# A written ScalarE order in the memory-attention stage of a fused two-layer kernel

## The chip, the cores and the metric

The kernel runs on one core of one Trainium2 chip. The metric is the device time of one execution in microseconds (us). Before the change it was 2856.61 us, the median of three runs (2856.53 to 2856.86).

The engines are named as the profile names them: PE is TensorE's matmul, PEld its weight load, DVE is VectorE, ACT is ScalarE, POOL is GpSimd, SP is SyncE.

## The reference, cut to what matters

The program adds six residual blocks to `x` (8 x 1024 x 256, float32), each after a layer norm: an FP4 feed-forward, an attention with decay, the FP4 feed-forward again, a ternary feed-forward, the memory attention, and the ternary feed-forward again. The change is in the memory attention (16 heads of 16, four memories):

```python
sq, sk = elu1(q), elu1(k)                     # elu1(x) = elu(x) + 1
out_m = einsum('bhsd,mhde->mbhse', sq, memories)
rel   = einsum('bhsd,mhd->mbhs', sq, memory_norms)
out_m = out_m / clip(rel, EPS, None)[..., None]
weights = softmax(rel.mean(axis=-1), axis=0)  # over the memories
mem_out = einsum('mbhse,mbh->bhse', out_m, weights)
kv_cum, k_cum = cumsum(sk x v), cumsum(sk)    # over the sequence
local = einsum('bhsd,bhsde->bhse', sq, kv_cum) / clip(sq . k_cum, EPS, None)
g = sigmoid(gate)
out = (g * mem_out + (1 - g) * local) @ w_o.T
x = x + out
```

## The kernel before, in words

**Tiling.** `x` stays on the chip. It is cut into NG = 16 groups of 512 rows, each of G = 4 tiles of 128 rows; two groups (GB = 2) or eight tiles (CB = 8) make one sequence. The stages run one after the other, and their ends overlap.

**The steps of memory attention.** `attn_memory` (the loop `for i in range(n + 5)`, n = 64) is a software pipeline by hand: step i works on tile i and on the five tiles before it, a = i-1 to e = i-5. With j = i mod 4, a step does in the code's order:

1. for tile b, memory product 0 (`remembered(0)`, tile pmo, L1410); for tile a, the four score products (`scored`, tile sc, L917), each for 32 of the 128 partitions; then memory products 1 to 3;
2. on VectorE, in between, the weighting of the memories (mo, L1423) and the masking of the scores (at, L926; the last one, `weigh_one(0)`, comes much later in the step);
3. for tile b, the product py (`recalled` L983, `weighed` L1001), copied to nt by ScalarE (L1515);
4. for tile a, the state (psd, then two ScalarE instructions, L1540); in each fourth step (j = 3) also the divisors of a later group (`divisors`: pr L1296, rt on ScalarE L1303 and on POOL L1304); the reciprocals rw (L1549);
5. the transposes of tiles d and c: pyt (L1565), copied by ScalarE to yt (L1567), and pn (L1572), from which VectorE makes y (L1575) and POOL adds four memories to it (L1582). In a fourth step pyt and pn are two halves of one bank, named pyn in the profile;
6. the running sum of the keys (kc, L1275), pieces of the layer-norm statistics (`ln.advance`, L206 to L228);
7. a projection of a later group (`project`: pk or pq, L1015; two ScalarE instructions to ee, L1255 and L1256; the ELU on VectorE, L1260), then the last masked score;
8. for tile e, the output product po (L1015); in a third step (j = 2) the transposes of the next group (`norm_turn`, L1235 and copies L1240);
9. `keys(i)`: for tile i, the transposed keys and the values in the tile pkv (L1378, L1015), and on ScalarE the copies vz (L1387) and kd (L1394) out of it and the two masked copies qz (L1398), which read sq alone; kd is left out in the last step of a sequence (i mod 8 = 7). The next step's scores read qz;
10. the ELU's last instruction, the addition of po to X (L1619), and in a second step (j = 1) the eight normalisations of a group (`norm`, L276 and L279).

A projection exists up to step 54.

**What sets the order.** The framework's scheduler orders the instructions of each engine; those handed to `pin` keep the order of the code on their engine. Before the change PE and DVE are pinned in this stage, ScalarE is not. PSUM has four banks that the stage calls `bank(0)` to `bank(3)` beside four score buffers.

**The statistics.** `statistics` cuts the layer-norm statistics into pieces: a mean and variance for each tile (L206, L207), and five pieces of terms for each batch of groups. `PLANS["memory"]` holds the batches and the step at which each is due. The first batch is done before the stage, in the last six groups of the ternary stage (`begin`); the others are spread over the steps before they are due. Before the change the batches have 3, 2, 3, 4 and 4 groups, due at 0, 1, 9, 21 and 37.

Of the kernel before, what the change touches and what calls it, by code (L numbers as in the profile page):

```python
# [9 lines left out]
F32 = mybir.dt.float32  # L10
# [7 lines left out]
P = 128  # L18
# [20 lines left out]
def macaron_kernel(  # L39
# [192 lines left out]
    def statistics(sizes, dues):  # L232

        mv = ln_pool.tile([P, NG * G, 2], F32, tag="ln_mv", name="ln_mv")
        lr = ln_pool.tile([P, NG * G], F32, tag="ln_r", name="ln_r")
        lb = ln_pool.tile([P, NG * G], F32, tag="ln_b", name="ln_b")

        def work(g0, size):  # L240

            out = []
            for n in range(G * g0, G * (g0 + size)):
                out.append(lambda n=n: tile_stats(X[n // G][:, n % G, :], mv[:, n, :]))
            n = slice(G * g0, G * (g0 + size))
            terms = []

            def term(k):
                if not terms:
                    terms.extend(norm_terms(mv[:, n, :], lr[:, n], lb[:, n]))  # L250
                terms[k]()

            return out + [lambda k=k: term(k) for k in range(5)]

        first, plan = [], {}
        begun = g0 = 0
        for size in sizes:
            size = min(size, NG - g0)
            if size <= 0:
                break  # L260
            shares, due = work(g0, size), dues[g0]
            if due <= begun:
                first += shares
            n, span = len(shares), due - begun
            for u in range(begun, due):
                plan[u] = shares[(u - begun) * n // span : (u + 1 - begun) * n // span]
            begun, g0 = due, g0 + size

        def advance(u):
            for share in plan.get(u, ()):  # L270
                share()

        def normalize(dst, g, only=None):
            for j in range(G) if only is None else (only,):
                n = G * g + j
                nc.scalar.activation(  # L276
                    dst[:, j, :], X[g][:, j, :], AF.Identity, bias=lb[:, n : n + 1]
                )
                nc.scalar.activation(dst[:, j, :], dst[:, j, :], AF.Copy, scale=lr[:, n : n + 1])  # L279

        return SimpleNamespace(
            mv=mv, lr=lr, first=first, advance=advance, normalize=normalize
        )
# [9 lines left out]
        "ternary": ((2, 2, 4, 4, 4), [max(0, g - 1) for g in range(NG)]),  # L293

        "memory": (
            (GB + 1, 2, 3, 4, NG), [max(0, G * (g - GB) - 3) for g in range(NG)]
        ),
    }
    begun = {}
# [902 lines left out]
    def attn_memory(after):  # L1202
        with ExitStack() as st:
# [18 lines left out]

            def norm(g):
                xn = xn_pool.tile([P, G, D], F32, tag="xn", name="xn")
                ln.normalize(xn, g)
                xns[g] = xn

            def norm_turn(g, banks, both_act=True):
                xt = bp.tile([P, 2, TG], F32, tag="xt", name="xt")
                xn = xns.pop(g)  # L1230
                for k in range(2):
                    pt = bank(banks[k], [P, TG], "pt")
                    for j in range(G):
                        pin(
                            nc.tensor.transpose(  # L1235
                                pt[:, j * P : (j + 1) * P], xn[:, j, k * P : (k + 1) * P], ident
                            )
                        )
                    if k == 0 or both_act:
                        nc.scalar.copy(xt[:, k, :], pt)  # L1240
                    else:
                        pin(nc.vector.tensor_copy(xt[:, k, :], pt))
                sq = bp.tile([P, 2, TG], F32, tag="sq", name="sq")
                sk = bp.tile([P, 2, TG], F32, tag="sk", name="sk")
                proj[g] = (xt, sq, sk)

            def project(g, m, of_q, pp):

                xt, sq, sk = proj[g]
                w, dst = (wq, sq) if of_q else (wkv, sk)  # L1250
                whole(
                    pin, pp, [(w[:, k, m * P : (m + 1) * P], xt[:, k, :]) for k in range(2)]
                )
                ee = lnp.tile([P, TG], F32, tag="ee", name="ee")
                nc.scalar.activation(ee, pp, AF.Relu, scale=-1.0)  # L1255
                nc.scalar.activation(ee, ee, AF.Exp, scale=-1.0)  # L1256

                def elu():
                    pin(
                        nc.vector.scalar_tensor_tensor(  # L1260
                            dst[:, m, :], pp, 0.0, ee, ALU.max, ALU.add
                        )
                    )
# [21 lines left out]
            def divisors(g, pr):  # L1285
# [17 lines left out]
                nc.scalar.activation(rt, pr[0 : NR + 32, :], AF.Identity, accum_out=su)  # L1303
# [4 lines left out]
            def weigh(b):  # L1308
# [21 lines left out]
                def exponents():  # L1330
# [11 lines left out]
                    nc.scalar.activation(lg, lg, AF.Exp)  # L1342

                def shares():
                    sm = cp.tile([P, 8, 2], F32, tag="sm", name="sm")
# [20 lines left out]

                return total, turned, exponents, shares

            def keys(i):
                g, j = divmod(i, G)  # L1370
                xt, sq, sk = proj[g][:3]
                cols = slice(j * P, (j + 1) * P)
                pkv = bank(3, [P, 2, D], "pkv")
                carried = (i + 1) % CB != 0
                if carried:
                    for m in range(2):
# [10 lines left out]
                nc.scalar.copy(  # L1387
                    vz[:, :, 0::2, :],
                    pkv[:, 1, :].rearrange("p (r e i) -> p r e i", e=2, i=HD),
                )  # L1390
                kd = None
                if carried:
                    kd = cp.tile([P, D], F32, tag="kd", name="kd")
                    nc.scalar.copy(kd, pkv[:, 0, :])  # L1394

                qz = cp.tile([P, 2, 2, P], F32, tag="qz", name="qz")
                for e in range(2):
                    nc.scalar.activation(  # L1398
                        qz[:, :, e, :], sq[:, :, cols], AF.Copy, scale=pm[:, e : e + 1]
                    )  # L1400
                chunk[i] = (vz, kd, qz)

# [30 lines left out]
            for i in range(n + 5):  # L1433
# [3 lines left out]
                if i == 0:  # L1437

                    waiting = []
                    for u in range(min(GB + 1, NG)):  # L1440
# [3 lines left out]
                        for v in range(G if u < GB else 1):  # L1444
                            pp = ps_s.tile([P, TG], F32, tag="sc", name="pq" if v % 2 else "pk")
                            waiting.append((project(u, v // 2, v % 2 == 1, pp), u, v))
                            if u < GB and u + 1 < NG:
                                ln.normalize(xns[u + 1], u + 1, v)
# [58 lines left out]
                if 0 <= b < n:  # L1507
# [7 lines left out]
                    nc.scalar.copy(nt, py)  # L1515
                    chunk[b] = (nt, mo, rw_b)
                if 0 <= a < n:

# [8 lines left out]
                if 0 <= a < n:  # L1527
# [8 lines left out]
                    if kd is not None:  # L1536

                        grown = sp.tile([P, 2, 2, HD], F32, tag="state", name="state")
                        for e_ in range(2):
                            nc.scalar.activation(  # L1540
                                grown[:, :, e_, :], pst[:, :, e_, :], AF.Copy,
                                scale=pm[:, e_ : e_ + 1],
                            )
                        if before is not None:
                            nc.gpsimd.tensor_tensor(grown, grown, before, ALU.add)
# [16 lines left out]
                if 0 <= d < n:  # L1562
                    y = ys.pop(d).rearrange("p (m h) i -> p m (h i)", m=2)
                    for m in range(2):
                        pin(nc.tensor.transpose(pyt[:, m, :], y[:, m, :], ident))  # L1565
                    yt = cp.tile([P, 2, P], F32, tag="yt", name="yt")
                    nc.scalar.copy(yt, pyt)  # L1567
                    ys[d] = yt
                if 0 <= c < n:
                    nt, mo_c, rw_c = chunk.pop(c)  # L1570
                    for m in range(2):
                        pin(nc.tensor.transpose(pn[:, m, :], nt[:, m, :], ident))  # L1572
                    y = cp.tile([P, H, HD], F32, tag="y", name="y")
                    pin(
                        nc.vector.tensor_tensor(  # L1575
# [14 lines left out]

                if "sum" in held:
                    running_sum(*held.pop("sum"))
                if i < n:
                    ln.advance(i)
                last = t + 1 if j == 3 else t
                elu = None
                if i < n and last < NG:
# [4 lines left out]
                weigh_one(0)  # L1602
                if 0 <= a < n:
                    chunk[a] = (vz, [ats[r] for r in range(4)], before, rw)
                if 0 <= e < n:
                    yt = ys.pop(e)
                    po = bank(1, [P, D], "po")
                    whole(pin, po, [(yt[:, m, :], wo[:, m, :]) for m in range(2)])
                if i < n and i % CB == 0:
                    mixing[1](bank(0, [P, NR], "pl"))  # L1610
                if i < n and j == 2 and t + 1 < NG:
                    norm_turn(t + 1, (3, 0))
                if i < n:
# [69 lines left out]
```

## Time and profile before

| what | value |
|---|---|
| median of three runs | 2856.61 us |
| the profiled execution | 2854.04 us |
| its span | 2851.3 us |
| mean granted TensorE clock | 0.984 |
| PE busy, 1972.1 to 2494.1 us | 484.5 of 522.0 us |
| DVE busy, 1972.1 to 2494.1 us | 422.1 of 522.0 us |
| ACT busy, 1972.1 to 2494.1 us | 268.4 of 522.0 us |
| POOL busy, 1972.1 to 2494.1 us | 252.7 of 522.0 us |

Times inside the profile are counted from the start of its span. The stretch in the table runs from the end of step 0's value products to that of step 55. A group's line says engine, source line, operation, output tile and input tiles. A wait's line says who waited for whom, the sum, the number of times and the longest.

### The profile page before, as it was taken

The page shows a single profiled execution, that of the slowest core. Times are in us where ns is not written, and L with a number is a line of the kernel's source. Part 1 is how long each engine was busy: PE and PEld are TensorE (multiplying, and loading weights), DVE is VectorE, ACT ScalarE, POOL GpSimd, SP SyncE. Part 2 cuts the span into 40 slices and gives each one's busy share as a digit, 9 for nine tenths or more (in the row PEclk, how much of TensorE's full clock was granted, in tenths as well). Part 3 has the DMA queues.
Part 4 walks back from the last instruction along what each step waited for, and adds up shares of the span by engine and source line. Part 5 has one row for each costly group of instructions (what it writes and reads, how often), then busy time and mean ns, then how long its engine had stood idle before and what let it go on. Part 6 is the DMA issues. An engine that isn't in the chain of part 4 may idle for free.

```text
span 2851.3 us, 53491 instructions
## 1 busy us (share of the span) xinstructions
PE 2644.8 (93%) x21536; PEld 1996.1 (70%) x21536; DVE 2089.3 (73%) x4732; ACT 1367.7 (48%) x3000; POOL 814.1 (29%) x760
## 2 busy tenths in 40 slices
PE   3779999999999998999999999998999999988999
PEld 2557777776676666677776779995666666667998
DVE  7787878776666667887878778555788877877654
ACT  3534444444434333444444456565455555435665
POOL 4434444430000002444444410001455455531000
PEclk9889999999999999999999999999999999999999
DMA  5100000000000000000000000000000000000011
GB/s 166 32 17 1 1 1 1 1 1 1 2 2 2 2 2 1 1 1 1 1 1 1 1 1 1 1 1 1 2 2 2 2 2 2 2 2 16 30 38 38
DMA packets 26228, 27.04 MB, mean 9 GB/s; under 512 B 5116, under 2 KB 25084, under 8 KB 25980
## 3 DMA queue, kind: packets, MB, share of 16 engines
q1 hardware_dynamic: 24838, 21.66, 2.4%
q8 instruction: 169, 2.77, 0.4%
q10 hardware_dynamic: 998, 1.44, 0.2%
q14 instruction: 79, 0.65, 0.1%
q0 software_dynamic: 144, 0.52, 0.1%
HBM read 15.23 MB, written 8.39 MB: 8 GB/s over the span
## 4 chain that ended last, share of the span: by engine, by line
PE 72%; DVE 16%; POOL 4%; ACT 4%; issue 2%; DMA 0%; POOLq 0%; DVEq 0%; ACTq 0%
PE po L874 9%; PE po L727 8%; PE ph L848 8%; PE pg L685 7%; PE pu L685 7%; PE py L1001 4%; PE sc L917 4%; PE po L1015 4%; PE pk L1015 4%; PE pkv L1015 3%; PE pq L1015 3%; DVE h L656 3%; PE py L983 2%; DVE qp L636 2%; DVE xn L656 1%
## 5 line engine op out<-in xcount | busy, mean ns | idle before, releaser
L727 PE MATMUL po<-wd,ht 128*128 128x256 f32 (+1 forms) x1536 | 359.9, 384 | 7.0 <-DVE x L736 6.5
L685 PE MATMUL pu<-wu,xt 128*128 128x352 f32 x1024 | 348.9, 463 | 11.0 <-DVE h L695 10.8
L685 PE MATMUL pg<-wg,xt 128*128 128x352 f32 x1024 | 348.5, 462 | 6.5 <-ACT sg L694 6.0
L727 PEld LDWEIGHTS po<-wd,ht 128*128 128x128 f32 (+1 forms) x1536 | 285.7, 193 | 45.1 <-DVE x L736 8.3
L660 POOL TENSOR_TENSOR h<-h,q_sc 128x704 f32<-128x704 f32 x128 | 177.5, 1387 | 451.9 <-DVE h L656 451.9
L685 PEld LDWEIGHTS pu<-wu,xt 128*128 128x128 f32 x1024 | 193.3, 192 | 114.5 <-DVE h L695 11.9
L695 DVE TENSOR_TENSOR h<-sg,pu 128x352 f32<-128x352 f32 x256 | 129.7, 516 | 187.4 <-PE pu L685 179.8
L685 PEld LDWEIGHTS pg<-wg,xt 128*128 128x128 f32 x1024 | 194.6, 191 | 100.2 <-ACT sg L694 10.9
L874 PE MATMUL po<-w,hl 128*128 128x256 f32 x1024 | 250.5, 282 | 1.1 <-DVE hl L859 1.1
L874 PE MATMUL po<-w,hh 128*128 128x256 f32 x1024 | 249.8, 282 | 0.0
L1582 POOL TENSOR_TENSOR y<-y,mo 128x256 f32<-128x256 f32 x256 | 210.2, 821 | 131.6 <-DVE y L1575 117.9
L656 DVE SCALAR_TENSOR_TENSOR h<-qp,h 128x704 f32<-128x704 f32 x256 | 227.2, 888 | 18.4 <-ACT qp L653 13.9
L859 DVE TENSOR_TENSOR hl<-hf,hh 128x512 fp32r<-128x512 f32 x256 | 168.0, 686 | 64.7 <-ACT hh L857 60.4
L848 PE MATMUL ph<-xh,w 128*128 128x512 f32 x512 | 203.6, 399 | 0.9 <-DVE x L1619 0.5
L694 ACT ACTIVATE sg<-pg 128x352 f32<-128x352 f32 x256 | 118.2, 462 | 177.7 <-PE pg L685 177.7
L848 PE MATMUL ph<-xl,w 128*128 128x512 f32 x512 | 200.6, 393 | 0.0
L644 POOL TENSOR_TENSOR h<-h,q_rs 128x704 f32<-128x704 f32 x128 | 177.6, 1387 | 71.4 <-DVE q_rs L640 54.2
L874 PEld LDWEIGHTS po<-w,hl 128*128 128x128 f32 x1024 | 195.0, 190 | 2.4 <-DVE hl L859 1.7
L874 PEld LDWEIGHTS po<-w,hh 128*128 128x128 f32 x1024 | 194.3, 190 | 1.8
L926 DVE TENSOR_TENSOR at<-sc,tri 128x512 f32<-128x512 f32 x256 | 171.4, 670 | 20.3 <-PE py L1001 17.2
L856 ACT ACTIVATE hf<-ph,b1c 128x512 f32<-128x512 f32 x256 | 167.7, 701 | 17.5 <-PE ph L848 17.4
L926 DVE TENSOR_TENSOR at<-sc,dec 128x512 f32<-128x512 f32 x256 | 158.5, 681 | 18.9 <-PE sc L917 18.9
(257 smaller groups left out, 5576.6 us busy)
## 6 DMA issues: line engine op xcount, KB each, us to landing
x<-in_x SPq DMA_DIRECT2D x15, 512.0 KB, 8.9
out<-x SPq DMA_DIRECT2D x15, 512.0 KB, 2.9
raw_w<-in_w_t SPq DMA_DIRECT2D x2, 1024.0 KB
wqkv<-in_wqkv_t SPq DMA_DIRECT2D x1, 768.0 KB
wu_n<-in_w_up ACTq DMA_DIRECT2D x2, 352.0 KB
wg_n<-in_w_gate SPq DMA_DIRECT2D x2, 352.0 KB
wd_n<-in_w_down ACTq DMA_DIRECT2D x1, 704.0 KB, 14.4
x<-in_x POOLq DMA_DIRECT2D x1, 512.0 KB, 10.9
```

The lines of the kernel that those rows point to most:

```text
L644: nc.gpsimd.tensor_tensor(vb, vb, rs[:, :, None].to_broadcast([P, nb, 16]), ALU.mult)
L656: nc.vector.scalar_tensor_tensor(v, mg, FP4_LEAST, v, ALU.max, op)
L660: nc.gpsimd.tensor_tensor(vb, vb, sc[:, :, None].to_broadcast(list(vb.shape)), ALU.mult)
L685: nc.tensor.matmul(ps, lhsT=xt[:, k, j * P : (j + 1) * P], rhs=w[:, k, cols], start=(k == 0), stop=(k == 1),)
L727: nc.tensor.matmul(po, lhsT=ht[:kn, c, :], rhs=wd[:kn, c, :], start=(c == 0), stop=(c == len(DCH) - 1),)
L848: nc.tensor.matmul(ph, lhsT=w1[:, k, f * P : (f + 1) * P], rhs=xt[:, k, :], start=(k == 0 and xt is xh), stop=(k == 1 and xt is xl),)
L856: nc.scalar.activation(hf, ph, AF.Gelu, bias=b1c[:, f : f + 1])
L859: nc.vector.tensor_tensor(hl[:, f, :], hf, hh[:, f, :].bitcast(F32), ALU.subtract)
L874: nc.tensor.matmul(po, lhsT=ht[:, f, j * P : (j + 1) * P], rhs=w2[:, f, :], start=False, stop=(f == NF - 1 and ht is hl),)
L926: nc.vector.tensor_tensor(at, sc.rearrange("p m (e t) -> p (m e) t", e=2), weight, ALU.mult)
L1015: nc.tensor.matmul(dst, lhsT=lhsT, rhs=rhs, start=n == 0, stop=n == len(parts) - 1)
L1582: nc.gpsimd.tensor_tensor(yv, yv, mo_c[:, :, :, m, :].rearrange("p r c n -> p c r n"), ALU.add)
```

## The change

All of it is in `attn_memory`, `normalize` and the plan. No arithmetic is changed.

- Every ScalarE instruction of the stage goes through `pin`, so ScalarE keeps the code's order too: in `normalize` (by a new argument), `norm_turn`, `project`, `divisors`, the exponents, `keys`, nt, the state and yt.
- The transposes pn come before the copy yt.
- `ln.advance(i)` moves from before the projection to behind the addition to X.
- The plan has batches of 5, 3, 4 and 4 groups, so that two more groups are done before the stage.
- In steps without a projection, the output product comes behind `keys` and not ahead of it, and pkv is in bank 2.

```diff
-            (GB + 1, 2, 3, 4, NG), [max(0, G * (g - GB) - 3) for g in range(NG)]
+            (GB + 3, 3, 4, NG), [max(0, G * (g - GB) - 3) for g in range(NG)]
...
-            def keys(i):
+            def keys(i, at):
...
-                pkv = bank(3, [P, 2, D], "pkv")
+                pkv = bank(at, [P, 2, D], "pkv")
...
                 vz = vzs[i % 4]
-                nc.scalar.copy(
-                    vz[:, :, 0::2, :],
-                    pkv[:, 1, :].rearrange("p (r e i) -> p r e i", e=2, i=HD),
+                pin(
+                    nc.scalar.copy(
+                        vz[:, :, 0::2, :],
+                        pkv[:, 1, :].rearrange("p (r e i) -> p r e i", e=2, i=HD),
+                    )
                 )
                 kd = None
                 if carried:
                     kd = cp.tile([P, D], F32, tag="kd", name="kd")
-                    nc.scalar.copy(kd, pkv[:, 0, :])
+                    pin(nc.scalar.copy(kd, pkv[:, 0, :]))
 
                 qz = cp.tile([P, 2, 2, P], F32, tag="qz", name="qz")
                 for e in range(2):
-                    nc.scalar.activation(
-                        qz[:, :, e, :], sq[:, :, cols], AF.Copy, scale=pm[:, e : e + 1]
+                    pin(
+                        nc.scalar.activation(
+                            qz[:, :, e, :], sq[:, :, cols], AF.Copy, scale=pm[:, e : e + 1]
+                        )
                     )
...
-                    yt = cp.tile([P, 2, P], F32, tag="yt", name="yt")
-                    nc.scalar.copy(yt, pyt)
-                    ys[d] = yt
                 if 0 <= c < n:
                     nt, mo_c, rw_c = chunk.pop(c)
                     for m in range(2):
                         pin(nc.tensor.transpose(pn[:, m, :], nt[:, m, :], ident))
+                if 0 <= d < n:
+                    yt = cp.tile([P, 2, P], F32, tag="yt", name="yt")
+                    pin(nc.scalar.copy(yt, pyt))
+                    ys[d] = yt
...
-                if i < n:
-                    ln.advance(i)
...
-                if 0 <= e < n:
+                def output():
                     yt = ys.pop(e)
                     po = bank(1, [P, D], "po")
                     whole(pin, po, [(yt[:, m, :], wo[:, m, :]) for m in range(2)])
+                    return po
+
+                if elu and 0 <= e < n:
+                    po = output()
...
                 if i < n:
-                    keys(i)
+                    keys(i, 3 if elu else 2)
                 if elu:
                     elu()
+                elif 0 <= e < n:
+                    po = output()
                 if 0 <= e < n:
                     xe = X[e // G][:, e % G, :]
                     pin(nc.vector.tensor_tensor(xe, po, xe, ALU.add))
+                if i < n:
+                    ln.advance(i)
```

More of the change, by code (lines that the diff above doesn't have):

```diff
@@ L271, in advance, with normalize @@
                 share()
-        def normalize(dst, g, only=None):
+        def normalize(dst, g, only=None, pin=lambda ins: ins):
             for j in range(G) if only is None else (only,):
                 n = G * g + j
-                nc.scalar.activation(
-                    dst[:, j, :], X[g][:, j, :], AF.Identity, bias=lb[:, n : n + 1]
-                )
-                nc.scalar.activation(dst[:, j, :], dst[:, j, :], AF.Copy, scale=lr[:, n : n + 1])
+                pin(
+                    nc.scalar.activation(
+                        dst[:, j, :], X[g][:, j, :], AF.Identity, bias=lb[:, n : n + 1]
+                    )
+                )
+                pin(
+                    nc.scalar.activation(
+                        dst[:, j, :], dst[:, j, :], AF.Copy, scale=lr[:, n : n + 1]
+                    )
+                )
         return SimpleNamespace(
@@ L1224, in norm @@
                 xn = xn_pool.tile([P, G, D], F32, tag="xn", name="xn")
-                ln.normalize(xn, g)
+                ln.normalize(xn, g, pin=pin)
                 xns[g] = xn
@@ L1239, in norm_turn @@
                     if k == 0 or both_act:
-                        nc.scalar.copy(xt[:, k, :], pt)
+                        pin(nc.scalar.copy(xt[:, k, :], pt))
                     else:
@@ L1254, in project @@
                 ee = lnp.tile([P, TG], F32, tag="ee", name="ee")
-                nc.scalar.activation(ee, pp, AF.Relu, scale=-1.0)
-                nc.scalar.activation(ee, ee, AF.Exp, scale=-1.0)
+                pin(nc.scalar.activation(ee, pp, AF.Relu, scale=-1.0))
+                pin(nc.scalar.activation(ee, ee, AF.Exp, scale=-1.0))
                 def elu():
@@ L1302, in divisors @@
                 su = bp.tile([NR + 32, 1], F32, tag="su", name="su")
-                nc.scalar.activation(rt, pr[0 : NR + 32, :], AF.Identity, accum_out=su)
+                pin(nc.scalar.activation(rt, pr[0 : NR + 32, :], AF.Identity, accum_out=su))
                 nc.gpsimd.tensor_scalar(rt, rt, EPS, 1.0, ALU.max, ALU.mult)
@@ L1341, in exponents @@
                     )
-                    nc.scalar.activation(lg, lg, AF.Exp)
+                    pin(nc.scalar.activation(lg, lg, AF.Exp))
                 def shares():
@@ L1386, in keys @@
                 vz = vzs[i % 4]
-                nc.scalar.copy(
-                    vz[:, :, 0::2, :],
-                    pkv[:, 1, :].rearrange("p (r e i) -> p r e i", e=2, i=HD),
+                pin(
+                    nc.scalar.copy(
+                        vz[:, :, 0::2, :],
+                        pkv[:, 1, :].rearrange("p (r e i) -> p r e i", e=2, i=HD),
+                    )
                 )
@@ L1393, in keys @@
                     kd = cp.tile([P, D], F32, tag="kd", name="kd")
-                    nc.scalar.copy(kd, pkv[:, 0, :])
+                    pin(nc.scalar.copy(kd, pkv[:, 0, :]))
                 qz = cp.tile([P, 2, 2, P], F32, tag="qz", name="qz")
                 for e in range(2):
-                    nc.scalar.activation(
-                        qz[:, :, e, :], sq[:, :, cols], AF.Copy, scale=pm[:, e : e + 1]
+                    pin(
+                        nc.scalar.activation(
+                            qz[:, :, e, :], sq[:, :, cols], AF.Copy, scale=pm[:, e : e + 1]
+                        )
                     )
@@ L1447, in attn_memory @@
                             if u < GB and u + 1 < NG:
-                                ln.normalize(xns[u + 1], u + 1, v)
+                                ln.normalize(xns[u + 1], u + 1, v, pin)
                             if len(waiting) > 1 or u == GB:
@@ L1514, in attn_memory @@
                     nt = cp.tile([P, 2, P], F32, tag="nt", name="nt")
-                    nc.scalar.copy(nt, py)
+                    pin(nc.scalar.copy(nt, py))
                     chunk[b] = (nt, mo, rw_b)
@@ L1539, in attn_memory @@
                         for e_ in range(2):
-                            nc.scalar.activation(
-                                grown[:, :, e_, :], pst[:, :, e_, :], AF.Copy,
-                                scale=pm[:, e_ : e_ + 1],
+                            pin(
+                                nc.scalar.activation(
+                                    grown[:, :, e_, :], pst[:, :, e_, :], AF.Copy,
+                                    scale=pm[:, e_ : e_ + 1],
+                                )
                             )
@@ L1572, in attn_memory @@
                         pin(nc.tensor.transpose(pn[:, m, :], nt[:, m, :], ident))
+                if 0 <= d < n:
+                    yt = cp.tile([P, 2, P], F32, tag="yt", name="yt")
+                    pin(nc.scalar.copy(yt, pyt))
+                    ys[d] = yt
+                if 0 <= c < n:
                     y = cp.tile([P, H, HD], F32, tag="y", name="y")
```

## The prediction, made before the result was known

> **What bounds the kernel now.** I read the page first, then the busy times of a stretch, then TensorE's waits, then two timelines of one step. The profiled execution took 2854.04 us, of which 2851.3 us are the span; the three timed runs have a median of 2856.61 us, 2.57 us above it. I add differences to the median.
>
> ```profile
> PE 2644.8 (93%) x21536; PEld 1996.1 (70%) x21536; DVE 2089.3 (73%) x4732; ACT 1367.7 (48%) x3000; POOL 814.1 (29%) x760
> ```
>
> TensorE (PE) is the bound overall. The change touches memory attention and its statistics alone. Step 0's value products (pkv, L1015) end at 1972.1 us and those of step 55 at 2494.1 us; the busy times of that stretch:
>
> ```profile
> core 0: us, PE busy (x) PEld busy (x) DVE busy (x) ACT busy (x) POOL busy (x), PEclk, DMA share, GB/s
> 1972.10:2494.10 522.00, 484.51 (x6297) 337.66 (x6296) 422.12 (x974) 268.38 (x691) 252.67 (x313) 0.98 0.01 2
> ```
>
> So 55 steps take 522.0 us, 9.5 us each; TensorE is busy for 93% of it, VectorE for 81%, ScalarE for 51%. TensorE's waits in it (engine, waiting line, releaser, sum, times, longest):
>
> ```profile
> PE pyn L1572 <- ACT yt L1567: 12.7, 13, 1.0
> PE sc L917 <- DVE at L926: 7.3, 7, 1.7
> PE pk L1015 <- DVE sq L1260: 5.4, 1, 5.4
> PE pmo L1410 <- DVE lg L1328: 4.6, 4, 3.1
> PE py L983 <- DVE mo L1423: 3.5, 7, 0.9
> PE pkv L1378 <- ACT xt L1240: 3.2, 13, 0.3
> ```
>
> These are 36.7 us of true idling. I also made a floor out of the cleanest steps, from the distance between successive value products in TensorE's timeline: 7.84 us for a first step of four (2385.80 to 2393.64), 8.35 for each eighth step, which has the mixing weights too (2421.87 to 2430.22), 7.87 for a second step (2475.47 to 2483.34, step 54, which has a second step's work), 9.20 for a third (2402.30 to 2411.50; it has the transposes of the next group), and 9.60 for a fourth (10.59 from 2375.21 to 2385.80, less its 0.98 us wait for yt). Steps 1 to 55 give 7 x 7.84 + 6 x 8.35 + 14 x 7.87 + 13 x 9.20 + 7.87 + 14 x 9.60 = 477 us. So 522.0 - 477 = 45 us of the stretch is waiting or a half clock: that is all that any reordering can win there.
>
> **Which order ScalarE keeps now.** The four lines below are ScalarE's timeline after the value products of step 43, the next three TensorE's at the same place (start, us, engine, line, tiles).
>
> ```profile
> 2386.86 0.37 ACT L1387 COPY vz<-pkv 128x256 f32<-128x256 f32 x1 [0.69 <-PE pkv L1015]
> 2387.13 0.38 ACT L1394 COPY kd<-pkv 128x256 f32<-128x256 f32 x1
> 2388.37 0.91 ACT L1398 ACTIVATE qz<-sq,pm 128x256 f32<-128x256 f32 x2 [0.86 <-PE pmo L1410]
> 2390.14 0.37 ACT L1515 COPY nt<-py 128x256 f32<-128x256 f32 x1 [0.86 <-PE py L1001]
> ```
>
> ```profile
> 2385.80 1.03 PE L1015 MATMUL pkv<-wkv,xt 128*128 128x256 f32 x4
> 2386.76 0.37 PE L1410 MATMUL pmo<-memb,sq 32*128 32x128 f32 x1
> 2386.77 0.50 PE L917 MATMUL sc<-qz,sk 32*128 32x256 f32 x3
> ```
>
> The score products sc of the next step start at 2386.77, at the heel of the value products. They read qz, the two masked copies that `keys` writes last. The qz pair shown, at 2388.37, comes after those scores have begun, so it isn't theirs: it is the next step's, waiting only until its buffer is read. ScalarE has been running this pair about a step ahead of where the code writes it (in the timeline's beginning four such copies, from 1956.9, stand before the first vz at 1972.17). That lead is what lets TensorE pass from pkv to sc with no pause.
>
> **The change, part by part.**
>
> *Written ScalarE order.* No instruction is added, and no DMA on SP's, ScalarE's or POOL's queue is moved. The pins put vz, kd, qz, qz in this order behind each step's pkv; TensorE's own order (pkv, memory product 0, scores) is pinned already. So the scores of a step now wait for: vz starting 0.03 us after pkv's modelled end (2386.83 to 2386.86), 0.27 to kd, 0.27 to the next instruction (ScalarE passes from a kd at 2376.71 to a normalisation at 2376.98), 0.91 for the pair, and some 0.05 from a ScalarE end to TensorE's start (yt ends at 2382.67, pyn starts at 2382.72): 1.53 us after pkv's end, where they now start 0.06 before it. That is **1.59 us a step**. Only memory product 0 lies beside it. Queued behind are all of TensorE's later products, so VectorE's masked scores and POOL's sums come later too. Upper side: 1.59. Lower side: memory product 0 (four passes of about 0.11, 0.43 in all) leaves the score block, but the three other row groups still have 4 score and 4 memory passes each, so I take nothing off; if it counted in full, 1.16. It holds for the 55 steps with a projection (0 to 54); six of them have no kd (0.27 less): 55 x 1.59 - 6 x 0.27 = **+85.8 us**.
>
> In the second step of four the eight normalisations (L276, L279, 0.40 apart, 3.2 us) now stand between qz and nt. From the scores' start to the end of py are 3.27 us (2386.77 to 2390.04), so nt is not late; if that cover is gone, at most 0.3 x 13 = 4 us. What the order takes away: normalisations no longer sit in ScalarE's queue waiting for statistics, ahead of vz; pmo's 4.6 us wait (longest 3.1) follows from that.
>
> *Shared transposes ahead of their copies.* In 13 fourth steps pyt and pn share a bank, and TensorE sits 0.98 us between them until yt is copied. Now both pairs go first: **-12.7 us**. yt comes 0.3 later, hidden behind the 1.7 us projection that stands before po.
>
> *Statistics at a step's end; five groups before the stage.* Each tile costs VectorE 0.53 us (L206 and L207). Behind the X addition, they no longer hold up the last masked score (sc <- at, 7.3 us) or the ELU. The 13 pieces of step 0 ran from 1971.23 to 1978.35 and cost TensorE 5.4 us at pk, and then half a clock (four pk passes took 3.80 us at 1979.13 where a clean step has 1.72); they now run in the ternary stage's last groups, where VectorE is busy for 24.8 of 60 us (1900 to 1960) and TensorE for 57.7. I cost them at nothing there; were the cover gone, 7.1 us.
>
> *Keys ahead of the last output products.* From step 55 there is no projection. po (1.03 us) then covers most of the qz wait, and po's own wait for the reciprocal (about 0.6 a step) moves off. These steps already turn in 7.87 us on a circle through POOL's four additions (3.15 us), mo, py and y, with TensorE idle about 0.7 before py; I take 0, between -5 and +4.
>
> **The sum.** If the 1.59 us pause makes every other wait of the stretch vanish (none but step 1's and three of 1.7 to 3.1 is longer, and those have their cause removed), then 85.8 - 45 = **+41 us**. The clock comes on top. In these slices the granted clock is the third number from the right (0.50 is half):
>
> ```profile
> 2011.68:2015.09 3.41, 2.21 (x38) 1.68 (x35) 3.34 (x10) 0.69 (x3) 3.00 (x4) 1.00 0.00 0
> 2015.09:2018.51 3.42, 3.42 (x65) 2.84 (x58) 1.53 (x4) 1.19 (x6) 0.32 (x1) 0.50 0.03 7
> ...
> 2318.87:2322.29 3.42, 1.77 (x20) 1.00 (x18) 3.25 (x9) 0.58 (x3) 2.44 (x3) 1.00 0.00 0
> 2322.29:2325.70 3.41, 3.34 (x80) 2.74 (x80) 2.88 (x9) 2.48 (x7) 1.27 (x1) 1.00 0.01 2
> ```
>
> A gap of 1.20 us before a score product (at 2013.45) was followed by a 3.4 us slice at half clock; one of 1.72 (at 2322.36) was not. Those gaps stood among thin score products; the new pause stands behind 3.7 us of dense ones (projection, po, pkv). Bounds: 0 to 37 such slices (two of three such gaps, of 55), each losing at most 1.7 us, 0 to 63 us; I take 4, near 0: +7.
>
> The page "TensorE: Matmul & The Clock Gate" of the Trainium skill, in its section "HAM oscillation — how this bites in real kernels", asks only that gaps stay under about 3.4 us. By that rule the new pauses would cost no clock and the sum would stay at +41; the slice at 2015.09 speaks against it.
>
> Forecast: 2856.61 + 41 + 7 = **2904 us** (+1.7%).
>
> **The rivals.**
>
> *The waits stay.* The pause moves VectorE and POOL with it, and only what is taken away by the edit itself goes (12.7 + 5.4): +68 us, with 8 half-clock slices (+14) +82: 2938. For it: y, its POOL additions and mo form a circle, and VectorE's share is high. Against: that circle turns in 7.87 us and a step would take 9.4.
>
> *The masked copies stay ahead: faster.* One mechanism, at L1398: if the scores find qz ready as they do now, the 45 us go and nothing comes: 2812. It decides at 45 / 55 = 0.82 us a step; under that pause the kernel is not slower. For it: ScalarE is idle half the time and qz needs nothing of pkv. Against: a queue in the written order can't reach qz before kd is done, and kd waits for pkv.
>
> *The order is not what changes:* pins that agree with the order already kept, 2857 within 6. Against: 1956.9 before 1972.17.
>
> **How the numbers follow.** Forecast 0.70 (own range 2874 to 2923: pauses of 1.16 us and no slice give +17, ten slices, the late nt and the tail's 4 give +66), waits stay 0.17, masked copies ahead 0.08, no change 0.05. 8 in 10 asks for the first two almost whole: 2874 to 2938. Slower by over 0.2% (5.7 us, about what a measurement can tell from no change) 0.87, within it 0.05, faster 0.08.
>
> **What would show it.** In the changed profile qz follows kd at 0.27 us and no longer waits for PE; a new wait "sc <- ACT qz" of about 1.5 us stands some 55 times; pyn <- yt and the 5.4 us at pk are gone; a plain step takes 9.4 us; VectorE's share falls. I am wrong if sc still starts at pkv's end, or if most slices behind a pause run at half clock (then up to 2960).

## The result, and the profile after

The changed kernel takes 2902.59 us (median of 4 runs, 2900.68 to 2903.37), the kernel before in the same comparison 2856.74 us: a ratio of 1.0158, 95% interval 1.0141 to 1.0176. The profiled execution took 2902.0 us, with a span of 2900.3 us and a mean granted clock of 0.984, the same clock as before.

The page's line of busy times, then the busy times of the stretch from the end of step 0's value products to that of step 55 (the columns are those of the same table before):

```profile
PE 2670.1 (92%) x21536; PEld 2018.9 (70%) x21536; DVE 2092.4 (72%) x4717; ACT 1369.9 (47%) x3000; POOL 812.7 (28%) x760
```

```profile
1980.10:2536.90 556.80, 495.94 (x6290) 350.42 (x6289) 418.80 (x938) 268.97 (x691) 249.79 (x311) 1.00 0.01 2
```

No engine has more instructions. The 55 steps take 556.8 us, where they took 522.0. Of the 34.8 us more, 23.4 are idle time of TensorE and 11.4 busy time (495.94 against 484.51): memory product 0, which ran among the scores, now runs alone in front of them. VectorE is busy for 418.80 / 556.80 = 75% of them, down from 81%. The clock in the stretch is 1.00, up from 0.98. TensorE's waits in the stretch (sum, times, longest):

```profile
PE sc L923 <- ACT qz L1407: 48.9, 55, 1.5
PE pn L1581 <- ACT nt L1525: 4.5, 12, 0.6
PE pkv L1384 <- ACT xt L1246: 3.8, 13, 1.0
PE py L989 <- DVE mo L1433: 3.1, 4, 1.1
```

One new wait stands 55 times, and four of the six old lines are gone: pyn for yt, sc for the masked scores, pk for the ELU, pmo for lg. Those for xt (3.8 us) and mo (3.1 us) stay, and one for nt (4.5 us) is new. ScalarE's timeline behind the value products of a plain step, then TensorE's at the same place:

```profile
2428.17 0.37 ACT L1394 COPY vz<-pkv 128x256 f32<-128x256 f32 x1 [0.69 <-PE pkv L1021]
2428.43 0.38 ACT L1402 COPY kd<-pkv 128x256 f32<-128x256 f32 x1
2428.70 0.92 ACT L1407 ACTIVATE qz<-sq,pm 128x256 f32<-128x256 f32 x2
2433.03 0.37 ACT L1525 COPY nt<-py 128x256 f32<-128x256 f32 x1 [3.42 <-PE py L1007]
```

```profile
2427.10 1.03 PE L1021 MATMUL pkv<-wkv,xt 128*128 128x256 f32 x4
2428.06 0.71 PE L1420 MATMUL pmo<-memb,sq 32*128 32x128 f32 x4
2429.67 1.17 PE L923 MATMUL sc<-qz,sk 32*128 32x256 f32 x16 [0.90 <-ACT qz L1407]
```

The qz pair now follows kd and waits for nothing but its turn. The value products end at 2427.10 + 1.03 = 2428.13 and the scores start 1.54 us later, where they used to start 0.06 us before that end: 1.60 us a step. So it is in 46 of the 55 steps. The six steps without kd have 1.32 or 1.33, and three of the first five have 1.66 to 1.75. The wait's own sum (48.9) is smaller than 55 x 1.60 because it counts only true idling; the 0.71 us of memory product 0 lie beside it.

Where the difference lies, from the ends of the value products in both traces (the two profiled executions, 48.0 us apart; the medians are 45.9 apart):

| part of the span | before | after | difference |
|---|---|---|---|
| up to step 0's value products | 1972.1 | 1980.2 | +8.0 |
| steps 1 to 55 | 522.0 | 556.7 | +34.7 |
| steps 56 to 63 | 64.6 | 67.5 | +2.9 |
| the rest | 292.6 | 295.9 | +3.3 |
| span | 2851.3 | 2900.3 | +49.0 |

The first row lies in the loop ahead of step 0. Its new wait, in TensorE's waits from 1930 to 1980 us:

```profile
PE pt L1241 <- ACT xn L282: 6.9, 4, 3.0
```

The transposes of the first groups wait for normalisations that ScalarE now takes in the code's order, behind other work of that loop.

### The profile page after: what moved, and what is told of

The parts are those of the page before. It is cut to its first block, busy times and chain, and to the rows that moved or that the text cites. A ratio compares the mean times of both kernels' runs of the same rounds, so it can differ in the third digit from the quotient of the medians.

```text
span 2900.3 us, 53369 instructions
## 1 busy us (share of the span) xinstructions
PE 2670.1 (92%) x21536; PEld 2018.9 (70%) x21536; DVE 2092.4 (72%) x4717; ACT 1369.9 (47%) x3000; POOL 812.7 (28%) x760
## 3 DMA queue, kind: packets, MB, share of 16 engines
q10 hardware_dynamic: 998, 1.44, 0.2%
## 4 chain that ended last, share of the span: by engine, by line
PE 71%; DVE 14%; ACT 8%; POOL 4%; issue 2%; DMA 0%; POOLq 0%; DVEq 0%; ACTq 0%
PE po L880 8%; PE po L733 8%; PE ph L854 8%; PE pg L691 7%; PE pu L691 7%; PE py L1007 4%; PE sc L923 4%; PE pk L1021 4%; PE po L1021 4%; PE pkv L1021 4%; PE pq L1021 3%; DVE h L662 3%; DVE qp L642 2%; PE py L989 2%; DVE xn L662 1%
## 5 line engine op out<-in xcount | busy, mean ns | idle before, releaser
L862 ACT ACTIVATE hf<-ph,b1c 128x512 f32<-128x512 f32 x256 | 167.3, 698 | 17.5 <-PE ph L854 17.4
```

Of the source, the lines that this page charges most:

```text
L862: nc.scalar.activation(hf, ph, AF.Gelu, bias=b1c[:, f : f + 1])
```

## The experiments

Times are medians; each ratio is to the kernel before, measured beside it on the same chip. "First step" to "fourth step" are the steps with j = 0 to 3, as in the prediction; their lengths are means over steps 12 to 52. The kernel before had medians of 2856.74 to 2857.64 us beside the runs, so differences between runs of different comparisons carry about 1 us. The theory tested first: the pause behind kd is the whole loss, and it hides the waits of before.

### 1. The masked copies a step earlier

The changed kernel, with the pair of qz for step i + 1 written behind the scores of step i:

```diff
+            def masks(i):
...
                 for r in (...):
                     scored(r)
+                if i == 0:
+                    masks(0)
+                if i + 1 < n:
+                    masks(i + 1)
```

> The changed kernel with the masked copies qz written (and pinned) one step earlier, behind the score products of the step before, where ScalarE ran them before the change; nothing else differs. Theory (the pause of 1.59 us between the value products and the scores, at 55 steps, is the loss): 86 us go, about 10 of VectorE's and POOL's waits come back, so about 2826 us, and no wait of sc for qz. Rival (the written order as a whole costs, by nt, state, rt and yt): under half of it goes, above 2860.

Measured: 2867.32 us, ratio 1.0032 (1.0020 to 1.0045). The pause is gone, and 35.3 of its 86 us come back. In its place, in the same stretch (525.4 us long), two other waits stand:

```profile
PE py L989 <- DVE mo L1440: 26.9, 29, 2.2
PE pn L1592 <- ACT nt L1536: 17.1, 12, 2.1
```

The second is the eight normalisations of a second step, which stand ahead of nt (in one step they run from 2180.32 on, and nt starts at 2184.91): in the changed kernel the pause held up py as well, so they cost less there (4.5 us). The first is a wait of before (3.5 us there) that has grown. So the pause costs time, but less than its length: something else was waiting behind it.

### 2. The masked copies ahead of vz and kd

The changed kernel, with the pair written first in `keys`, so that it runs while TensorE is still at the value products:

```diff
+                qz = cp.tile([P, 2, 2, P], F32, tag="qz", name="qz")
+                for e in range(2):
+                    pin(nc.scalar.activation(qz[:, :, e, :], ...))
                 vz = vzs[i % 4]
...
-                qz = cp.tile([P, 2, 2, P], F32, tag="qz", name="qz")
-                for e in range(2):
-                    pin(nc.scalar.activation(qz[:, :, e, :], ...))
```

> The changed kernel with qz written ahead of vz and kd inside keys; ScalarE stays pinned. Theory: qz then ends 2.2 us after the start of the ELU's first copy, some 0.3 us behind the value products in three steps of four and not at all in a third step, so about 15 of the 86 us stay and about 2840 us result. Rival (the copies vz and kd, now later, become the late ones): state products wait, and it stays above 2860.

Measured: 2855.26 us, ratio 0.9993 (0.9984 to 1.0003). One place in the queue is worth 47.3 us, the whole loss, and yet 15 us less than the expectation. In its profile, of an execution of 2860.19 us, steps 1 to 55 take 514.4 us, 7.6 less than before; step 0's value products still end 7.1 us later than before, and steps 56 to 63 take 68.2 us, 3.6 more. TensorE's largest wait in steps 1 to 55:

```profile
PE py L989 <- DVE mo L1433: 21.2, 28, 2.2
```

Again py's wait for the weighted memories. Its cause is looked for in the fifth, ninth and twelfth run.

### 3. The pause alone

The kernel before, with only vz, kd and qz pinned:

```diff
-                nc.scalar.copy(vz[:, :, 0::2, :], ...)
+                pin(nc.scalar.copy(vz[:, :, 0::2, :], ...))
...
-                    nc.scalar.copy(kd, pkv[:, 0, :])
+                    pin(nc.scalar.copy(kd, pkv[:, 0, :]))
...
-                    nc.scalar.activation(qz[:, :, e, :], ...)
+                    pin(nc.scalar.activation(qz[:, :, e, :], ...))
```

> The kernel before with only vz, kd and qz pinned on ScalarE, nothing else of the change. Theory: the pause of 1.59 us comes alone (+86 us), and the waits of VectorE for POOL and of TensorE for at and mo, 27 of the 45 us, vanish behind it: about 2915 us. Rival (these waits stay beside the pause): about 2942 us. Third view (the loss needs the whole ScalarE order): near 2857 us.

Measured: 2924.97 us, ratio 1.0235 (1.0219 to 1.0250). The three pins alone cost 67 us, more than the whole change, between the theory's 2915 us and the rival's 2942. TensorE's waits in the stretch:

```profile
PE sc L917 <- ACT qz L1401: 53.1, 52, 3.5
PE pyn L1576 <- ACT yt L1571: 12.7, 13, 1.0
PE pmo L1414 <- DVE lg L1328: 4.6, 4, 3.1
...
PE py L983 <- DVE mo L1427: 0.2, 1, 0.2
```

The wait for mo vanishes behind the pause without any edit to it; those for yt and lg stay whole. So the pause swallows some of the old waits, and the rest of the change had to take away the others.

### 4. Output products behind the keys in every step

The changed kernel, with po always behind `keys`, so that 1 us of TensorE's work covers most of the pause:

```diff
-                if elu and 0 <= e < n:
-                    po = output()
...
                 if elu:
                     elu()
-                elif 0 <= e < n:
+                if 0 <= e < n:
                     po = output()
```

> The changed kernel with the output products po behind keys in every step, not in the last ones alone, so that 1.03 us of TensorE work lie between the value products and the scores. Theory: the pause falls from 1.59 to 0.56 us at 55 steps, 57 us less: about 2846 us. Rival (the pause isn't what bounds, or the later addition to X delays memory product 1, which shares its bank with po): 2890 us or more.

Measured: 2876.96 us, ratio 1.0066 (1.0051 to 1.0081), 25.6 us faster than the changed kernel instead of 57. The expectation was too high from the start: of the pauses only 48.9 us were idle, the rest already held memory product 0. In its stretch sc waits for qz only 5.4 us (5 times), but pkv waits 12.4 us for xt, 13 times: by the code's order, po was what covered the copies of the next group's transposes in each third step. And py waits 8.3 us for mo.

### 5. The shared transposes alone

The kernel before, with the transposes pn ahead of the copy yt:

```diff
                         pin(nc.tensor.transpose(pyt[:, m, :], y[:, m, :], ident))
-                    yt = cp.tile([P, 2, P], F32, tag="yt", name="yt")
-                    nc.scalar.copy(yt, pyt)
-                    ys[d] = yt
                 if 0 <= c < n:
...
                         pin(nc.tensor.transpose(pn[:, m, :], nt[:, m, :], ident))
+                if 0 <= d < n:
+                    yt = cp.tile([P, 2, P], F32, tag="yt", name="yt")
+                    nc.scalar.copy(yt, pyt)
+                    ys[d] = yt
```

> The kernel before with the shared transposes ahead of the copy yt, and nothing else of the change. Theory of the prediction (the 0.98 us wait at 13 fourth steps is on the path): 12.7 us less, about 2844 us. Rival, formed after the first runs (in a fourth step POOL does rt, the state and four additions, 5.4 us, before the next step's mo can be written, so TensorE only meets the wait one step later, before py): pyn no longer waits for yt, but py waits for mo some 0.7 us more in each first step; 2853 to 2857 us.

Measured: 2854.16 us, ratio 0.9988 (0.9979 to 0.9997): 2.8 us and not 12.7. The edit did what it says: the wait for yt is gone, and a fourth step takes 9.34 us instead of 10.54, 13 x 1.20 = 15.6 us less. But the first step behind it takes 9.10 us instead of 8.09, 13 x 1.01 = 13.1 us more. POOL's timeline across that boundary, then VectorE's line and TensorE's line behind it:

```profile
2384.45 1.92 POOL L1304 TENSOR_SCALAR rt<-rt 96x512 f32<-96x512 f32 x1 [3.91 <-ACT rt L1303]
2386.45 0.32 POOL L1545 TENSOR_TENSOR state<-state 128x64 f32<-128x64 f32 x1
2386.73 3.15 POOL L1584 TENSOR_TENSOR y<-y,mo 128x256 f32<-128x256 f32 x4
```

```profile
2389.91 0.42 DVE L1423 TENSOR_TENSOR mo<-pmo,rw 128x256 f32<-128x256 f32 x1 [1.57 <-POOL y L1584]
```

```profile
2390.39 0.64 PE L983 MATMUL py<-sq,state 32*32 32x128 f32 x16 [0.82 <-DVE mo L1423]
```

In a fourth step POOL clips rt (1.92 us) ahead of the state and the four additions. The additions end at 2389.88, VectorE's mo follows, and only then py. TensorE arrives sooner and waits for POOL instead of for yt: py's waits for mo rise from 3.5 to 11.5 us. This chain, which runs from one step into the next, is what is called POOL's circle below.

### 6. The statistics alone

The kernel before, with the new batches and the pieces at the step's end:

```diff
-            (GB + 1, 2, 3, 4, NG), ...
+            (GB + 3, 3, 4, NG), ...
...
-                if i < n:
-                    ln.advance(i)
...
                     pin(nc.vector.tensor_tensor(xe, po, xe, ALU.add))
+                if i < n:
+                    ln.advance(i)
```

> The kernel before with the new plan (five groups ahead of the stage) and the statistics at a step's end, and nothing else of the change. Theory of the prediction: the 5.4 us wait at pk and its half clock go (about 5 us in all), and the 7.3 us of sc waiting for at: about 2845 us. Rival (the statistics' later place holds up mo of the next step, and py with it): py waits for mo more by what sc waits less; about 2852 us.

Measured: 2843.68 us, ratio 0.9950 (0.9938 to 0.9963), 13.2 us faster. Nothing shows in the ternary stage: step 0's value products end at 1971.6 us (1972.1 before). The waits at pk (5.4 us), for the last masked score (7.3, now 0.3) and of pmo for lg (4.6) are gone, the last with ScalarE still free. But another has grown from 3.5 us, as the rival said:

```profile
PE py L983 <- DVE mo L1423: 17.6, 22, 2.2
```

So TensorE idles almost as long as before in steps 1 to 55 (36.4 us, 37.5 before). The profiled stretch is 10.4 us shorter, and 8.4 of that lie in steps 1 to 4: step 1, with the wait at pk and the half clock behind it, took 12.65 us and now takes 4.43. In steps 5 to 55 the profile shows a gain of 2.1 us. The first part of the theory holds; the masked scores' 7.3 us were not won, their place was taken by mo.

### 7. The first loop's normalisations free

The changed kernel, with the normalisations of the loop ahead of step 0 left to the scheduler:

```diff
-                                ln.normalize(xns[u + 1], u + 1, v, pin)
+                                ln.normalize(xns[u + 1], u + 1, v)
```

> The changed kernel with the normalisations of the loop ahead of step 0 not pinned on ScalarE; all else as changed. Theory (written between the ELU's copies they come late for the transposes: pt waits 6.9 us for xn, and step 0's value products end 8.0 us later than before): 6.5 us of that come back, about 2896 us. Rival (the 8 us come from the two more groups of statistics ahead of the stage): no difference, 2902 us.

Measured: 2897.26 us, ratio 1.0138 (1.0124 to 1.0152): 5.3 us less than the changed kernel. Step 0's value products end at 1972.3 us again. So the +8.0 us of the table's first row is this pin; the steps gave 2.8 us of it back (559.5 against 556.7 us).

### 8. Masked copies first, normalisations in halves

The second kernel with the first loop free, the eight normalisations split over the second and third step behind yt, and po ahead of the keys again:

```diff
-                ln.normalize(xn, g, pin=pin)
+                for v in (2 * q, 2 * q + 1):
+                    ln.normalize(xns[g], g, v, pin)
...
-                if elu and 0 <= e < n:
+                if 0 <= e < n:
                     po = output()
...
-                    keys(i, 3 if elu else 2)
+                    keys(i, 3)
```

> As the run with qz first (2855 us), and with: the first loop's normalisations not pinned; a group's eight normalisations written in halves behind yt in the second and third steps, in place of all behind qz; po ahead of keys in the last steps again. Theory (pn waits for nt in third steps, the first loop and the last steps cost 6, 6.5 and 3 us): about 2840 us. Rival (POOL's circle, rt, state, four additions, mo, py, sets the step and takes back what is won elsewhere): 2848 us or more.

Measured: 2851.54 us, ratio 0.9977 (0.9968 to 0.9987), 3.7 us less than the second kernel. The steps keep their mean lengths (first step 9.08 us, 9.09 in the second kernel; third step 10.15, 10.21), and py still waits 21 us for mo. Nor is ScalarE's order out of play:

```profile
PE sc L923 <- ACT qz L1396: 10.5, 10, 2.4
```

In each eighth step (i mod 8 = 1) the first half of the normalisations comes late, and qz behind it: the third step that follows takes some 10.5 us, every other one some 9.8, where the second kernel has 10.2 for both. What the halves won in one they lost in the other. In the profiles the gain lies outside: step 0's value products end 5.9 us sooner than in the second kernel and steps 56 to 63 take 4.6 us less, while steps 1 to 55 take 3.2 us more.

### 9. The transposes, with POOL's clipping late

The fifth kernel, with the clipping of rt behind the four additions on POOL:

```diff
-                nc.gpsimd.tensor_scalar(rt, rt, EPS, 1.0, ALU.max, ALU.mult)
+                clips.append(rt)
...
                         pin(nc.gpsimd.tensor_tensor(yv, yv, mo_c[...], ALU.add))
+                for rt_ in clips:
+                    pin(nc.gpsimd.tensor_scalar(rt_, rt_, EPS, 1.0, ALU.max, ALU.mult))
+                clips.clear()
```

> As the run of the kernel before with the transposes alone (2854 us), and POOL's clipping of rt (1.92 us, needed some steps later) written behind the four additions in fourth steps and pinned there. Theory (POOL's circle rt, state, additions, mo, py took back what the transposes won): the first step falls from 9.10 to about 8.0 us, 13 times, so about 2842 us. Rival (the first step is held by something else, VectorE's masked score or the state's copies): no change, 2854 us.

Measured: 2846.13 us, ratio 0.9961 (0.9948 to 0.9973). Against the kernel before, the transposes and the late clipping together are worth 11.1 us; the transposes alone were worth 2.8. The late clipping alone was not run. The first steps fell from 9.10 to 8.79 us, a third of what they had lost, which is 4.0 of the 8.0 us between the two medians. Where the rest comes from is open: in the profiles the stretch is 5.3 us shorter (516.3 us, 521.6 in the fifth kernel), with one half-clock slice fewer (at most 1.7 us), and 2.0 us lie ahead of step 0's value products.

### 10. Statistics, transposes and late clipping together, ScalarE free

The sixth kernel with the edits of the fifth and ninth. Nothing is pinned on ScalarE.

> The kernel before with the statistics' part (2843.7 us alone), the transposes and the late clipping of rt, ScalarE not pinned. Theory: the parts now add up, 13 and 12 us: about 2830 us. Rival (the statistics at a step's end delay mo by the same POOL and VectorE time, so the two gains overlap): 2838 us or more.

Measured: 2832.60 us, ratio 0.9914 (0.9900 to 0.9927), the fastest here, faster than both kernels of the case. The gains add up: 13.2 (run 6) + 11.1 (run 9) = 24.3 expected, 24.6 measured. What is left is still py behind mo (23.1 us, 29 times). VectorE's own waits in these steps name what mo waits for:

```profile
DVE mo L1428 <- POOL y L1590: 16.0, 22, 1.5
```

That is POOL's four additions (3.15 us), which read an older tile's mo: the pool these tiles come from has two buffers, so a new mo takes the buffer of two tiles before. The additions cannot start until the state, its reciprocal and y are there. A third buffer for mo was not tried.

### 11. A longer pause

The changed kernel, with the second masked copy of each pair written twice (the same values again):

```diff
-                for e in range(2):
+                for e in (0, 1, 1):
```

> The changed kernel with the second masked copy of each pair done twice (the same values, 0.40 us more ScalarE time between kd and the scores). Theory (at a pause of 1.59 us every other wait is already hidden, so a longer pause is paid in full): 55 x 0.40 = 22 us more, about 2925 us, a plain step 9.83 us. Rival (something else beside the pause bounds a step): 2910 us or less.

Measured: 2965.15 us, ratio 1.0375 (1.0359 to 1.0390), 62.6 us above the changed kernel and not some 22. The pause grew by 0.54 us and not 0.40 (in one step the value products end at 2179.53 and the scores start at 2181.61, 2.08 behind), which is 55 x 0.54 = 30 us. The other half is the clock, which the theory had left out. The whole stretch, and two neighbouring slices in it (the third number from the right is the granted clock):

```profile
1979.20:2602.70 623.50, 535.69 (x6289) 380.03 (x6289) 420.37 (x938) 296.96 (x746) 249.46 (x311) 0.92 0.01 2
```

```profile
2179.30:2182.70 3.40, 1.96 (x26) 1.58 (x27) 1.33 (x5) 1.96 (x5) 2.14 (x4) 1.00 0.00 0
2182.70:2186.10 3.40, 3.40 (x60) 2.65 (x59) 1.78 (x4) 0.00 (x0) 0.00 (x0) 0.50 0.02 5
```

The first holds a whole pause: 3.40 - 1.96 = 1.44 us of idle TensorE. The next runs at half clock. 28 such slices stand in the stretch, one in the changed kernel. TensorE is busy for 535.69 us with the products it did in 495.94.

### 12. The eighth kernel, with the clipping late

The eighth kernel with the edit of the ninth.

> The kernel of the eighth run, with GpSimd's clipping of rt written and pinned behind the four additions of the state. Theory (the circle over GpSimd, rt, state, additions, mo, took back what the earlier qz had given): without the 1.92 us of rt ahead of the additions py's waits for mo fall from 20.8 us to some 10 and the time to about 2842 us. Rival (these waits are given back elsewhere, or the second masked copy bounds the step): 2851 us, as in the eighth run.

Measured: 2846.91 us, ratio 0.9965 (0.9951 to 0.9979), 4.6 us less, half of what the theory asked. py's waits for mo fall from 21.0 to 17.4 us, the first steps from 9.08 to 8.76. The clipping is a part of the circle; the larger part of these waits has another cause, for which run 10's line (additions, then mo) is the best sign.

## Why the prediction was right, point by point

*The pause: right.* 1.59 us a step was worked out; 1.60 was measured at 46 of the 55 steps, and 1.32 or 1.33 at the six without kd, for which 1.32 was worked out. qz follows kd at 0.27 us as named, and a plain first step takes 9.43 us, which is 7.84 + 1.59. Taking it away by one place in the queue (run 2) brings the time back to that of before; adding it alone (run 3) costs 67 us.

*"Every other wait of the stretch vanishes": nearly right for the changed kernel.* Waits of 11.4 us beside the pause are left. From step 5 on, the steps take 522.2 us, and floor plus pause give 522.0. That is closer than its parts: the second and third steps are 0.2 us longer than floor plus pause, the fourth steps 0.3 shorter. The four first steps took 34.5 where floor plus pause give 40.9: the floor was too high there, because not all tiles of the pipeline exist yet. Runs 1, 2 and 4 show what this point left out: most of the waits are hidden and not removed. Filling the 86 us of pauses gave back 35 us (run 1) and 47 us (run 2); run 4, which could fill the 49 us of idle in them, gave back 26.

*pmo's wait of 4.6 us: gone, but for another reason.* The prediction put its going down to the written order. The statistics' edit is enough: it is gone in run 6 too, where ScalarE is free, and whole in runs 3 and 5, which lack the statistics' edit.

*nt: not late, said the prediction, and at most 4 us if its cover goes.* It is late: pn waits 4.5 us for it, 12 times, just above that bound.

*The shared transposes, -12.7 us: right inside the changed kernel, wrong as a price of its own.* The wait is gone, but alone the edit is worth 2.8 us (run 5), because the next step gives the time back to POOL's circle. The prediction knew such a circle, at 7.87 us a turn, but not that the 1.92 us of rt lengthen it in a fourth step.

*The statistics at nothing in the ternary stage: right.* Step 0's value products end no later in run 6. That its gain of 13.2 us is close to the two waits the prediction named (5.4 + 7.3) is chance: most of it comes from step 1, and what the masked scores gave up went to mo.

*Keys ahead of the last output products, 0, between -5 and +4: inside.* Steps 56 to 63 took 2.9 us more. po's wait for the reciprocal went as foreseen (4.5 us to 0.3), and py's wait for mo rose from 5.2 to 6.4. Two half-clock slices stand here (2542.0 and 2548.8), none before; they can be worth 3.4 us, all of the difference, and step 56 alone took 13.14 us instead of 9.02. In runs 8 and 12, with po ahead of the keys again, no such slice stands there and the steps take 63.6 and 63.2 us.

*The clock, +7: too high.* Four half-clock slices were taken, on top of a floor at full clock; the stretch has one, at most 1.7 us, where the kernel before had six (20.5 us in all). A pause that leaves 0.90 us of idle did not trip the clock, and the waits that stood in or ahead of the old slices (pk for the ELU, sc for the masked scores twice, pmo for lg) are gone. The upper bound was no fancy: run 11, 0.54 us further, has 28 such slices.

The page "TensorE: Matmul & The Clock Gate" of the Trainium skill puts the fall to half clock, in its section "HAM oscillation — how this bites in real kernels", at gaps over some 3.4 us. The changed kernel's pauses fit that, all but one, but run 11's 1.44 us gaps do not: the 28 half-clock slices of that stretch speak against the figure.

*What was not in the sum: the loop ahead of step 0.* The written order pins its normalisations too, and this was priced at nothing. It cost 8.0 us there, 5.3 us of the total (run 7). The last row of the table, +3.3 us behind the stage, was not foreseen either. It holds 13.6 us of half-clock slices against 10.2 before, at most 1.7 us of the 3.3; the rest stays open. Over all profiles this part took 292.1 to 296.7 us.

So the total, 2902.59 against 2904, is closer than its parts. The stretch came out 13 us lower than forecast (34.7 against 41 + 7): 6.4 by the first four steps, 7 by the clock. What lies outside it came out 14 us higher (8.0 + 2.9 + 3.3). The mechanism carries the result; the last few us agree by chance.

*The rivals.* "The waits stay" (2938) did not happen in the changed kernel. Run 3, the pause without the other edits, lies between (2924.97): the waits for mo and the masked scores went there, those for yt and lg stayed, and 3.8 us of the one at pk. "The masked copies stay ahead" (2812) was refuted for the change, and runs 1 and 2 make it happen: 2867 and 2855, not 2812. Its price was wrong for the same reason as the transposes': the 45 us are not free once the pause is gone.

## What to carry to other kernels

Before pinning an engine that was free, look in its timeline for instructions that run ahead of where the code writes them: writing the code's order down takes that lead away, and what it covered in front of the bounding engine then stands as a pause at every step (here 86 us, of which 67 were paid when nothing else was changed). A long regular pause hides the smaller waits of the same loop, so price an edit by the step it is in and the step behind it; what it frees may be handed to the next circle (here POOL's additions, mo, py). And when an order must be written by hand, write first what needs nothing of the step's own products.

## What the runs showed of the hardware that was not expected

In run 11 the clock falls at a sharp amount of idle time. Its stretch was cut into the 3.41 us slices of its granted clock; slices already at half clock were left out, and TensorE's idle time in each other was added up. Below 1.2 us of idle, none of 122 slices was followed by one at half clock; from 1.2 to 1.4 us 1 of 6; from 1.4 to 1.6 us 24 of 25; above, the only one. In the changed kernel's stretch none of the 35 slices with 0.8 to 1.0 us of idle was followed by one at half clock, and 1 of the 9 with 1.0 to 1.2 us. The edge is not the same in every mix of work: in run 1 neither of the two slices from 1.4 to 1.6 us was followed by half a clock, 1 of 4 from 1.6 to 1.8, and all 3 above; in the kernel before, slices with 1.20 and 1.60 us were, one with 1.65 was not. What besides idle time moves the edge was not tried, nor where in a slice a pause does least harm.

So 0.54 us more of pause cost 62.6 / 55 = 1.14 us a step: across this edge, the lengthening cost twice its length.
